# One copy of u for a graph's eight slots, two relus kept on ScalarE, and masks and counts on VectorE, in a two-layer graph network

## The chip, the cores and the metric

The kernel runs on one core of a Trainium2 chip. TensorE (PE in the profile, its weight loads PEld), VectorE (DVE), ScalarE (ACT) and GpSimd (POOL) each work through an instruction queue of their own, in order; SyncE (SP) issues most of the loads and stores. The metric is the device time of one execution in microseconds (us); lower is better.

## The reference, cut to what matters

There are 128 graphs of 128 nodes with 64 features. Layer 0 takes, for each node j, the sum over its neighbours k of a relu of a term of j plus a term of k. Layer 1 is a message pass with a GRU update. Each layer ends in a residual sum and a layer norm.

```python
# layer 0
mask = (adj > 0.0).astype(x.dtype)
h = relu((x @ W1a)[:, :, None, :] + (x[:, :, None, :] - x[:, None, :, :]) @ W1b + b1)
hm = einsum('bjkh,bjk->bjh', h, mask)          # H = 192
x = layernorm(x + hm @ W2 + sum(mask, -1)[..., None] * b2)
# layer 1
m = relu(relu(x @ W1 + b1) @ W2 + b2)
msg = relu(adj @ m)
r, z, n = gru_gates(msg, x)
x = layernorm(x + (1.0 - z) * n + z * x)
```

With u = x(W1a + W1b) + b1 and v = -x W1b, the term is relu(u[j] + v[k]).

## The kernel before

**Work and tiles.** The kernel takes 32 groups of four graphs (`G` = 4). A graph's neighbours are split into two halves of 64 (`K`), and each node's neighbours in a half are numbered by a running count (`ranks`, from the mask by a matmul). A node has eight first slots in each half (`W0` = 8); what goes beyond lies in segments of four (`W1` = 4), which `counts`, `offsets` and `places` lay out in 128 rows a graph. `own` says which node owns a segment row; it comes from `till` (L464), a comparison of a ramp with the running sum of segments, by a matmul of differences (L469) and two copies (L472, L474).

**Gathers.** `pick0` (L518) holds one-hot matrices: which neighbour fills slot c of node j. A gather (L633) is twelve matmuls of 64 rows: two slots (`C` = 2), two halves, and v as the sum of three bf16 pieces b0, b1, b2 (`pieces`, L567 to L576). It adds v of two slots of all 128 nodes to a PSUM tile of 128 x 2 x 2 x 192 that already holds u. ScalarE put it there: a seed (L603) copies u into all four places of the tile. The result is u[j] + v[k]. The first gather of a graph is read by ScalarE, which keeps relu of it in `acc` (L653); the later ones by VectorE, which adds their relu to `acc` (L663).

**How far one seed goes.** One tile is seeded for `CH` = 2 gathers. The second gather uses differences of picks (slot minus the slot two before, L532): it takes the old v out and puts the new one in, so it must wait until the first has been read. Four gathers of a graph take two seeds. The segment rows (t = 1) go by pairs of graphs: one seed from `us` (`over`, L614 and L620) for four gathers, by `pick1`. Three PSUM tiles (`ps_g`) take turns.

**Sums.** GpSimd folds `acc` in two steps and subtracts `nb`, the relu of u for the empty slots (`together`, L683 to L688, once a graph); `joined` (L696) does the segments' first step. `sums` (L708 to L726) turns both to feature rows hmT. `others` makes t4 = degree x b2 + x on GpSimd (L479, L481).

**Tail of a group.** `second` multiplies hmT by W2 (L283, L287), adds t4 (L291) and starts the layer norm: statistics on VectorE (L253, L255), eps, negated mean, power -0.5 and their product on GpSimd (L258 to L264), scale and shift on ScalarE (L268). `turn`, `message1` to `message3`, `gates` and `update` are layer 1; the update's four steps (L363 to L372) run on GpSimd, for the last group on VectorE. In the last group `filler` issues matmuls of zeros to an otherwise unused tile (L277).

**Order.** The order is written out: `TIMETABLE` gives each part of a group a due time per step, with 100000 units for one group, `FIRST` other ones for group 0, `SETUP` those of the constants. All steps are sorted by due time and issued so, each engine's queue in that order; steps of up to four groups alternate. The due times set the order only; waiting is by semaphores. The loads of a group (adjT L396, xT L402, x L404) go out on SP some two groups ahead. Behind the last group a check of the segment counts (L777 to L782) guards a slow path, which doesn't run here.

Of the kernel before, what the change touches and what calls it, by code (L numbers as in the profile page):

```python
# [8 lines left out]
F32 = mybir.dt.float32  # L9
# [6 lines left out]
N = 128  # L16
F = 64
# [7 lines left out]
CH = 2  # L25
# [6 lines left out]
    "load": (-239888,), "masks": (-238156,), "ranks": (-200576, -194850), "degrees": (-228408, -221484),  # L32
    "turned": (-189933, -183749), "counts": (-191910,), "offsets": (-181787, -175193, -172562, -162838, -161741),
    "owners": (820, 6053), "places": (-147612, -144441), "pieces": (-137076, -118201, -110813, -98096),
# [5 lines left out]
    "together3": (3714, 4697, 9068), "second": (29982, 34541, 34541, 44075, 44075, 45808), "turn": (49612, 49612),  # L40
    "message1": (55001, 56214), "message2": (57048, 57570), "message3": (65700, 77281),
    "gates": (83209, 86661, 89400, 92470, 92470, 92470),
    "update": (101744, 120595, 123001, 139151, 150290, 198413, 246921, 250824, 311612),
# [3 lines left out]
    "reduce": (-89041, -82113, -76359, -62977, -60541, -50033, -42948, -38936, -23485, -15405, -15405, -3453),  # L47
    "seed1": (-48740, -15516), "gather1": (-43978, -41686, -35644, -21221, -11810, -3717, 8136, 9311),
    "keep1": (-43301, -6818), "reduce1": (-37237, -25519, -20358, -3084, 8983, 10522),
# [3 lines left out]
SETUP = (-246768, -205868, -187652, -148058, -89840, 21303)  # L53
FIRST = {
    "load": (-190305, -108672), "masks": (-146596,), "ranks": (-129578, -128520), "degrees": (-138361, -133585),
    "turned": (-96218, -93766), "counts": (-124777,), "offsets": (-105877, -105577, -94566, -80587, -71431),
    "places": (-66249, -65974), "pieces": (-99801, -97830, -85303, -54033), "values0": (-105954, -105954, -105954),
    "values1": (-107124, -106310, -106310), "pick0": (-113119, -99973, -97396, -97396), "pick1": (-52074, -45312),
    "over0": (-59699, -52348),
# [4 lines left out]
def adj_resnorm_kernel(  # L64
    ctx: ExitStack,
    tc: tile.TileContext,
    x: bass.AP,
# [17 lines left out]
    NB = x.shape[1]  # L85
# [18 lines left out]
    iota = const.tile([N, N], BF16, name="iota")  # L104
# [4 lines left out]
    wall = const.tile([N, 2, 2 * H], F32, name="wall")  # L109
    b1o = const.tile([N, H], BF16, name="b1o")  # L110
# [37 lines left out]
    def turned_round(out, src):  # L148

        nc.scalar.copy(out[:, :, 0 : H - N], src[:, :, N:H])  # L150
        nc.scalar.copy(out[:, :, H - N : H], src[:, :, 0:N])

    def setup(ps_g, ps_w):
# [10 lines left out]
        for h in range(2):  # L164
            spread(bias[h * F : h * F + 3, 0:H], b1)
# [40 lines left out]
        turned_round(b1o.rearrange("p (c h) -> p c h", c=1), b1r.rearrange("p (c h) -> p c h", c=1))  # L206
# [15 lines left out]
        yield  # L222
        nc.vector.tensor_copy(bias[:, H : H + F], bi[:, 128:H])
        nc.vector.tensor_add(bias[:, H + F : 2 * H], bias[:, H + F : 2 * H], bi[:, 0:128])

# [15 lines left out]
    def tail_parts(s, work, ps_w, n, store):  # L241


        name = s["name"]

# [3 lines left out]
        def layernorm(y, tag, into):  # L249
# [4 lines left out]
            for i in range(n):  # L254
                nc.vector.bn_aggr(mv[:, i, :], stats[:, i, :])  # L255
            yield
            ve = work.tile([N, n], F32, tag="ve" + tag, name=f"ve{tag}_{name}")
            nc.gpsimd.tensor_scalar(ve, mv[:, :, 1], EPS, None, ALU.add)  # L258
            nm = work.tile([N, n], F32, tag="nm" + tag, name=f"nm{tag}_{name}")
            nc.gpsimd.tensor_scalar(nm, mv[:, :, 0], -1.0, None, ALU.mult)  # L260
# [3 lines left out]
            nc.gpsimd.tensor_tensor(nm, nm, rs, ALU.mult)  # L264
# [7 lines left out]
        def filler(n):  # L272

            if name == str(ng - 1):
                p = s["spare"]
                for i in range(n):
                    nc.tensor.matmul(p, ones_h, zeros, start=True, stop=True)  # L277

        def second():
            ps = [ps_w.tile([N, 2, F], F32, tag="w", name=f"pw{name}") for h in range(2)]  # L280
            hm = s["hmT"]
            for i in range(n):
                nc.tensor.matmul(ps[i % 2][:, i // 2, :], hm[:, i // 2, i % 2, :], w2c[:, 0, :], start=i < 2, stop=False)  # L283
            yield
            for i in range(n):
                hs = slice(i % 2 * F, (i % 2 + 1) * F)
                nc.tensor.matmul(ps[i % 2][:, i // 2, :], hm[hs, i // 2, 2, :], w2c[hs, 1, :], start=False, stop=i >= 2)  # L287
            yield
            y = work.tile([N, n, F], F32, tag="y0", name=f"y0_{name}")
            for h in range(2):  # L290
                nc.vector.tensor_add(y[:, h:n:2, :], ps[h], s["t4"][:, h:n:2, :])  # L291
            filler(9)
            yield from layernorm(y, "0", "x1")

        def turn():
            p = ps_w.tile([N, 2, N], F32, tag="w", name=f"pt{name}")
            for i in range(2):
# [3 lines left out]
            s["x1T"] = work.tile([N, 2, N], F32, tag="x1T", name=f"x1T{name}")  # L301
            nc.scalar.copy(s["x1T"], p)

        def message1():
            p = ps_w.tile([N, 2, N], F32, tag="w", name=f"pm{name}")
# [3 lines left out]
            s["m1"] = work.tile([N, 2, N], F32, tag="m1", name=f"m1_{name}")  # L309
            nc.scalar.activation(s["m1"], p, AF.Relu, bias=gb1)  # L310

        def message2():
            p = ps_w.tile([N, n, F], F32, tag="w", name=f"pn{name}")
            nc.tensor.matmul(p, ones_h, each(gb2, n), start=True, stop=False)
            for i in range(2):
                nc.tensor.matmul(p[:, 2 * i : 2 * i + 2, :], s["m1"][:, i, :], gw2, start=False, stop=i == 1)
# [5 lines left out]
        def message3():  # L322
            p = ps_w.tile([N, 2, N], F32, tag="w", name=f"pa{name}")
            for i in range(2):
# [564 lines left out]
```

## Time and profile before

| | |
|---|---|
| median of 3 runs | 984.29 us (983.44 to 986.48) |
| profiled execution: its time | 983.37 us |
| its span, first to last instruction | 981.5 us |
| busy in the span: PE, DVE, ACT, POOL | 898.1, 857.8, 841.0, 889.1 us |
| granted TensorE clock, mean | 0.984 |
| gathers L633 | 9216 matmuls, 481.6 us busy |
| relu and add L663 | 576 x 950 ns |
| seeds L603 from uv, from us | 256 x 807 ns, 64 x 807 ns |
| relus kept L653 | 192 x 810 ns |

A row of the profile names line, engine, operation, output and inputs by the program's names, shape and count, then busy time and the mean of one in ns; in brackets or behind a bar stand the idle time of the engine ahead of it and what ended that. A group is one 32nd of these counts. Timelines give start, length and line, with "x24" for instructions of a kind in a row.

### The profile page before, as it was taken

To read this page: it belongs to the slowest core of one execution; us is meant where nothing else is said; L and a number is where in the kernel's file an instruction comes from. 1 tells how busy PE (TensorE), PEld (TensorE's weight loads), DVE (VectorE), ACT (ScalarE), POOL (GpSimd) and SP (SyncE) were. 2 spreads that over 40 slices of the span, in tenths; PEclk is the share of its full clock that TensorE was granted. 3 is DMA by queue.
4 is the path that set the end of the run, shared out by engine and by line. 5 is a ranking of instruction groups with operands and counts; after the bars stand their busy time and mean duration, and the time that the engine had idled before them with its cause. 6 is when DMAs were issued, how large, how long until landed. Compare 5 with 4: busy or idle time off the path is not lost.

```text
span 981.5 us, 31854 instructions
## 1 busy us (share of the span) xinstructions
PE 898.1 (91%) x13015; PEld 703.1 (72%) x13015; DVE 857.8 (87%) x1617; ACT 841.0 (86%) x1708; POOL 889.1 (91%) x1171
## 2 busy tenths in 40 slices
PE   5789999999999999999999999999999999999984
PEld 2567777777777777777777777777777777777762
DVE  5888999888989989899988898998989998889962
ACT  4878889888889888888988888988888998888863
POOL 4658899999999999999999999999999999999963
PEclk6999999999999999999999999999999999999997
DMA  3000000001010001001000000001011000000000
GB/s 108 13 2 23 24 29 3 29 29 29 28 29 11 21 28 29 29 29 29 3 29 28 29 28 29 8 23 30 28 29 29 22 9 29 28 29 7 8 8 19
DMA packets 21459, 23.86 MB, mean 24 GB/s; under 512 B 4150, under 2 KB 17212, under 8 KB 21308
## 3 DMA queue, kind: packets, MB, share of 16 engines
q1 hardware_dynamic: 21308, 21.78, 7.4%
q8 instruction: 104, 1.70, 0.7%
q14 instruction: 47, 0.39, 0.1%
HBM read 17.57 MB, written 4.19 MB: 22 GB/s over the span
## 4 chain that ended last, share of the span: by engine, by line
PE 42%; POOL 36%; DVE 15%; issue 4%; ACT 2%; DMA 0%; DVEq 0%; SPq 0%; ACTq 0%; POOLq 0%
PE pv L633 19%; DVE acc L663 9%; POOL fs L688 6%; POOL acc L683 5%; POOL acc L696 5%; POOL acc L685 5%; POOL b L576 4%; PE pw L283 3%; PE pu L548 3%; POOL r L570 3%; PE ph L715 2%; PE pm L306 2%; PE pw L287 2%; POOL t L481 2%; DVE stats L253 2%
## 5 line engine op out<-in xcount | busy, mean ns | idle before, releaser
L663 DVE SCALAR_TENSOR_TENSOR acc<-pv,acc 128x768 f32<-128x768 f32 x576 | 534.4, 950 | 80.3 <-PE pv L633 63.7
L633 PE MATMUL pv<-b,pick 64*128 64x192 bf16 x9216 | 481.6, 244 | 37.1 <-DVE acc L663 14.9
L633 PEld LDWEIGHTS <-pick 64*128 64x128 bf16 x9216 | 379.1, 95 | 113.7 <-issue 86.2
L603 ACT COPY pv<-uv 128x768 f32<-128x768 f32 x256 | 204.2, 807 | 11.5 <-DVE acc L663 11.5
L653 ACT ACTIVATE acc<-pv 128x768 f32<-128x768 f32 x192 | 155.5, 810 | 23.9 <-PE pv L633 23.0
L683 POOL TENSOR_TENSOR acc<-acc 128x384 f32<-128x384 f32 x128 | 131.3, 1026 | 16.8 <-DVE acc L663 16.8
L685 POOL TENSOR_TENSOR acc<-acc 128x192 f32<-128x192 f32 x128 | 107.1, 836 | 2.7
L518 DVE TENSOR_TENSOR pick<-rankT,ramp 128x2048 bf16<-128x2048 bf16 x64 | 85.1, 1331 | 0.0
L688 POOL TENSOR_TENSOR fs<-acc,nb 128x192 f32<-128x192 f32 x128 | 75.2, 598 | 0.2
L726 ACT COPY hmT<-ph 128x384 f32<-128x384 f32 x64 | 31.1, 486 | 48.3 <-PE ph L720 48.3
L262 POOL TENSOR_TENSOR rs<-ve,nhalf 128x4 f32<-128x4 f32 x64 | 66.7, 1042 | 0.0
L696 POOL TENSOR_TENSOR acc<-acc 128x384 f32<-128x384 f32 x64 | 64.2, 1004 | 1.9 <-DVE acc L663 1.9
L576 POOL TENSOR_TENSOR b<-r,b 128x768 bf16<-128x768 f32 (+1 forms) x35 | 54.0, 1542 | 11.9 <-ACT b L573 11.9
L548 PE MATMUL pu<-wall,xT 64*128 64x384 f32 x256 | 60.8, 526 | 1.4 <-DVE larger L434 0.6
L614 PE MATMUL pz<-uv,own 128*128 128x192 f32 x256 | 58.9, 353 | 0.7 <-ACT own L474 0.7
L555 ACT COPY uv<-pu 128x384 f32<-128x384 f32 x128 | 55.1, 485 | 4.9 <-PE pu L551 4.8
L603 ACT COPY pv<-us 128x768 f32<-128x768 f32 x64 | 51.6, 807 | 6.9 <-DVE acc L663 6.8
L675 ACT ACTIVATE nb<-uv,npad 128x192 f32<-128x192 f32 x128 | 57.5, 450 | 0.0
L268 ACT ACTIVATE x<-y,nm,rs 128x64 f32<-128x64 f32 x128 | 45.9, 429 | 13.1 <-POOL nm L264 13.1
L570 POOL TENSOR_TENSOR r<-uv,b 128x768 f32<-128x768 f32 x31 | 51.1, 1650 | 3.3 <-ACT b L567 3.3
L414 POOL TENSOR_SCALAR maskT<-adjT 128x512 bf16<-128x512 f32 x32 | 49.1, 1535 | 5.1 <-DMA adjT<-in_adjT_dram 5.1
L715 PE MATMUL ph<-ownT,acc 128*128 128x128 f32 x256 | 42.1, 287 | 11.9 <-POOL acc L696 11.9
(150 smaller groups left out, 1746.4 us busy)
## 6 DMA issues: line engine op xcount, KB each, us to landing
adjT<-in_adjT_dram SPq DMA_DIRECT2D x32, 256.0 KB, 2.8
xT<-in_xT_dram SPq DMA_DIRECT2D x64, 64.0 KB, 2.8
x<-in_x_dram SPq DMA_DIRECT2D x32, 128.0 KB, 2.4
out_dram<-o SPq DMA_DIRECT2D x32, 128.0 KB, 1.7
wab<-in_w_dram SPq DMA_DIRECT2D x2, 96.0 KB, 2.5
bi<-in_b_ih_dram SPq DMA_DIRECT2D x1, 96.0 KB
bias<-in_b_hh_dram SPq DMA_DIRECT2D x1, 96.0 KB
wx<-in_w_hhT_dram SPq DMA_DIRECT2D x2, 48.0 KB, 2.7
```

What stands on the lines that cost most here:

```text
L518: nc.vector.tensor_tensor(s[name][:, rows], s[src].rearrange("p (o g) n -> p o g n", o=1).to_broadcast([N, n, G, N]), ramp[:, first : firs ...
L548: nc.tensor.matmul(ps[h], s["xT"][ks, i, :], wall[ks, i, :], start=True, stop=False)
L570: (nc.vector if g == 0 else nc.gpsimd).tensor_tensor(r[:, gs], v, b[0][:, gs], ALU.subtract)
L576: nc.gpsimd.tensor_tensor(b[2][:, gs], r[:, gs], b[1][:, gs], ALU.subtract)
L603: nc.scalar.copy(v, src.to_broadcast(list(v.shape)))
L633: nc.tensor.matmul(v[:, h, j, :], pick[ks], s[f"b{c}"][ks, gr, :], start=False, stop=c == 2, skip_group_check=True,)
L653: nc.scalar.activation(kept(s, t, i), view(s["pv", t, i, 0]), AF.Relu)
L663: nc.vector.scalar_tensor_tensor(out=a, in0=view(s["pv", t, i, k // CH if t == 0 else 0]), scalar=0.0, in1=a, op0=ALU.max, op1=ALU.add,)
L683: nc.gpsimd.tensor_tensor(f[:, 0], f[:, 0], f[:, 1], ALU.add)
L685: nc.gpsimd.tensor_tensor(f[:, 0, 0], f[:, 0, 0], f[:, 0, 1], ALU.add)
L688: nc.gpsimd.tensor_tensor(fs[:, i % 2], f[:, 0, 0], s["nb", i], ALU.subtract)
L696: nc.gpsimd.tensor_tensor(f[:, 0], f[:, 0], f[:, 1], ALU.add)
```

## The change

- **Seeds.** `CH` is 4: one seed for a graph's four gathers, so four instead of eight a group. The picks of the second to fourth gather are all differences, and one more set of them is computed.
- **Lift.** For graphs 1 and 3 of a group the last gather is not added by VectorE: ScalarE keeps its relu in a tile of its own (`lift`), and GpSimd adds that to `acc`.
- **Sums by pairs.** `together` works on two graphs in one instruction, twice as wide.
- **Mask, counts, layer norm.** The mask, the five counts, eps and the negated mean times the power move from GpSimd to VectorE; the negated mean is no step of its own any more.
- **Till and own.** `till` is the sign of a ramp plus offset, in four ScalarE activations; the two copies of own scale by a half and add a constant column `top`.
- **x.** It is not loaded a second time: the residual enters y by matmuls of xT with the identity; `others` loses its addition. Graphs alternate between the halves of xT, so the two copies of wall become one. Group 0's adjT and xT are loaded from ScalarE's queue ahead of its table load.
- **Update.** The z columns of weights and bias are negated, so that the gate gives 1 - z: y = (tanh - x1)(1 - z) + 2 x1, three steps instead of four, and 2 x1 on ScalarE.
- **Last group.** Its layer 1 runs in two pairs of graphs with parts of their own (`second_a` to `update_a`).
- The due times are all new, and some tiles have other buffer counts (fs, us, nb, acc0, lift).

The diff, without the tables of due times, the halved index ranges of `tail_parts` and the slow path:

```diff
-CH = 2
+CH = 4
+LIFT = (1, 3)
...
-        nc.vector.tensor_add(wall[:, 0, 0:H], wab[:, 0, :], wab[:, 1, :])
-        nc.vector.tensor_scalar_mul(wall[:, 0, H : 2 * H], wab[:, 1, :], -1.0)
-        turned_round(wall[:, 1, :].rearrange("p (c h) -> p c h", c=2), wall[:, 0, :].rearrange("p (c h) -> p c h", c=2))
-        nc.vector.tensor_copy(iota, ips)
+        nc.vector.tensor_add(wall[0:F, 0:H], wab[0:F, 0, :], wab[0:F, 1, :])
+        nc.vector.tensor_scalar_mul(wall[0:F, H : 2 * H], wab[0:F, 1, :], -1.0)
+        for o, c in ((0, slice(N, H)), (H - N, slice(0, N))):
+            k = c.stop - c.start
+            nc.vector.tensor_add(wall[F:N, o : o + k], wab[F:N, 0, c], wab[F:N, 1, c])
+            nc.vector.tensor_scalar_mul(wall[F:N, H + o : H + o + k], wab[F:N, 1, c], -1.0)
+        nc.vector.tensor_scalar(behind, ips, -1.0, -0.5, ALU.mult, ALU.add)
+        nc.vector.tensor_scalar_mul(top, ident[:, 0:1], 0.5)
...
+        nc.gpsimd.tensor_scalar(wm[:, 128:H], wm[:, 128:H], -1.0, None, ALU.mult)
+        nc.gpsimd.tensor_scalar(wx[:, F:128], wx[:, F:128], -1.0, None, ALU.mult)
...
-            yield
             ve = work.tile([N, n], F32, tag="ve" + tag, name=f"ve{tag}_{name}")
-            nc.gpsimd.tensor_scalar(ve, mv[:, :, 1], EPS, None, ALU.add)
-            nm = work.tile([N, n], F32, tag="nm" + tag, name=f"nm{tag}_{name}")
-            nc.gpsimd.tensor_scalar(nm, mv[:, :, 0], -1.0, None, ALU.mult)
+            nc.vector.tensor_scalar(ve, mv[:, :, 1], EPS, None, ALU.add)
+            yield
             rs = work.tile([N, n], F32, tag="rs" + tag, name=f"rs{tag}_{name}")
             nc.gpsimd.tensor_tensor(rs, ve, nhalf[:, 0:n], ALU.pow)
             yield
-            nc.gpsimd.tensor_tensor(nm, nm, rs, ALU.mult)
+            nm = work.tile([N, n], F32, tag="nm" + tag, name=f"nm{tag}_{name}")
+            nc.vector.scalar_tensor_tensor(out=nm, in0=mv[:, :, 0], scalar=-1.0, in1=rs, op0=ALU.mult, op1=ALU.mult)
             yield
             s[into] = work.tile([N, n, F], F32, tag=into, name=f"{into}_{name}")
             for i in range(n):
...
+                nc.tensor.matmul(ps[i % 2][:, i // 2, :], g["xT"][hs, (lo + i) // 2, :], ident[hs, hs], start=False, stop=False)
...
+            s["x2"] = work.tile([N, n, F], F32, tag="x2", name=f"x2{name}")
+            nc.scalar.mul(s["x2"], s["x1"], 2.0)
+            yield
-            side.tensor_tensor(a, s["x1"], t, ALU.subtract)
+            side.tensor_tensor(a, t, s["x1"], ALU.subtract)
             yield
             b = work.tile([N, n, F], F32, tag="ub", name=f"ub{name}")
             side.tensor_tensor(b, a, s["rz"][:, :, F:128], ALU.mult)
             yield
-            c = work.tile([N, n, F], F32, tag="uc", name=f"uc{name}")
-            side.tensor_tensor(c, b, t, ALU.add)
-            yield
             y = work.tile([N, n, F], F32, tag="y1", name=f"y1_{name}")
-            side.tensor_tensor(y, c, s["x1"], ALU.add)
+            side.tensor_tensor(y, b, s["x2"], ALU.add)
             yield
             yield from layernorm(y, "1", "o")
...
-                nc.sync.dma_start(s["adjT"], adjT[:, gs, :])
+                q = nc.scalar if g == 0 else nc.sync
+                q.dma_start(s["adjT"], adjT[:, gs, :])
...
-                    nc.sync.dma_start(s["xT"][h * F : (h + 1) * F], xT[:, g * G + 2 * h : g * G + 2 * h + 2, :])
-                s["x"] = loads.tile([N, G, F], F32, tag="x", name=f"x{g}")
-                nc.sync.dma_start(s["x"], x[:, gs, :])
+                    q.dma_start(s["xT"][h * F : (h + 1) * F], xT[:, g * G + h : (g + 1) * G : 2, :])
...
-                nc.gpsimd.tensor_scalar(s["maskT"], s["adjT"], 0.0, None, ALU.is_gt)
+                nc.vector.tensor_scalar(s["maskT"], s["adjT"], 0.0, None, ALU.is_gt)
...
-                nc.gpsimd.tensor_scalar(up, s["larger"], 1.0 / W1, less - float(W0) / W1, ALU.mult, ALU.add)
+                nc.vector.tensor_scalar(up, s["larger"], 1.0 / W1, less - float(W0) / W1, ALU.mult, ALU.add)
+                yield
...
-                nc.vector.tensor_tensor(
-                    s["till"], each(iota, G), off.rearrange("p (g o) -> p g o", o=1).to_broadcast([N, G, N]), ALU.is_lt
-                )
+                for i in range(G):
+                    nc.scalar.activation(s["till"][:, i, :], behind, AF.Sign, bias=off[:, i : i + 1])
...
-                nc.scalar.copy(s["own"], s["po"])
+                nc.scalar.activation(s["own"], s["po"], AF.Identity, bias=top, scale=0.5)
                 s["own32"] = prep.tile([N, G, N], F32, tag="own32", name=f"own32_{g}")
-                nc.scalar.copy(s["own32"], s["po"])
+                nc.scalar.activation(s["own32"], s["po"], AF.Identity, bias=top, scale=0.5)
 
...
-                nc.gpsimd.tensor_tensor(s["t4"], s["t4"], s["x"], ALU.add)
...
-                v = s["pick0"].rearrange("p (q h c) g n -> p q h c g n", q=2, h=2)
-                for q in range(2):
-                    nc.vector.tensor_tensor(v[:, q, 1], v[:, q, 1], v[:, q, 0], ALU.subtract)
+                for a, b in ((C, 2 * C), (2 * C, W0)):
+                    nc.vector.tensor_tensor(p[:, W0 - C + a : W0 - C + b], p[:, a:b], p[:, a - C : b - C], ALU.subtract)
...
-                        pick, gr = (s["pick1"][:, k and W1 - 1 + k, 2 * i + j, :], 2 * i + j) if t else (s["pick0"][:, C * k + j, i, :], i)
+                        pick, gr = (s["pick1"][:, k and W1 - 1 + k, 2 * i + j, :], 2 * i + j) if t else (s["pick0"][:, k and W0 - C + C * k + j or j, i, :], i)
...
-                    if k:
+                    if k and not (t == 0 and k == nu[0] - 1 and i in LIFT):
...
+        def lift(s, i):
+
+            def part():
+                r = s["lift", i] = main.tile([N, 2, C, H], F32, tag="lift", name=f"lift{s['g']}", bufs=2)
+                nc.scalar.activation(r, view(s["pv", 0, i, 0]), AF.Relu)
+                yield
+
+            return part
+
         def base(s, i):
 
             def part():
-                nb = s["nb", i] = main.tile([N, H], F32, tag="nb", name=f"nb{s['g']}")
-                nc.scalar.activation(nb, s["uv"][:, i, 0:H], AF.Relu, scale=s["npad"][:, i : i + 1])
-                yield
-
-            return part
-
-        def together(s, i):
-            def part():
-                f = kept(s, 0, i)
-                nc.gpsimd.tensor_tensor(f[:, 0], f[:, 0], f[:, 1], ALU.add)
-                yield
-                nc.gpsimd.tensor_tensor(f[:, 0, 0], f[:, 0, 0], f[:, 0, 1], ALU.add)
-                yield
-                fs = made(s, ("fs", i // 2), main, [N, 2, H], F32, tag="fs", name=f"fs{s['g']}")
-                nc.gpsimd.tensor_tensor(fs[:, i % 2], f[:, 0, 0], s["nb", i], ALU.subtract)
+                nb = made(s, ("nb", i // 2), main, [N, 2, H], F32, tag="nb", name=f"nb{s['g']}", bufs=3)
+                nc.scalar.activation(nb[:, i % 2], s["uv"][:, i, 0:H], AF.Relu, scale=s["npad"][:, i : i + 1])
+                yield
+
+            return part
+
+        def together(s, q):
+            def part():
+                f = s["acc0", q]
+                for i in range(2):
+                    if 2 * q + i in LIFT:
+                        nc.gpsimd.tensor_tensor(f[:, i], f[:, i], s["lift", 2 * q + i], ALU.add)
+                        yield
+                nc.gpsimd.tensor_tensor(f[:, :, 0], f[:, :, 0], f[:, :, 1], ALU.add)
+                yield
+                nc.gpsimd.tensor_tensor(f[:, :, 0, 0], f[:, :, 0, 0], f[:, :, 0, 1], ALU.add)
+                yield
+                fs = s["fs", q] = main.tile([N, 2, H], F32, tag="fs", name=f"fs{s['g']}", bufs=2)
+                nc.gpsimd.tensor_tensor(fs, f[:, :, 0, 0], s["nb", q], ALU.subtract)
                 yield
 
             return part
...
-            parts = {"load": loading(s), **prep_parts(s), **tail_parts(s, work, ps_w, G, storer(g))}
+            parts = {"load": loading(s), **prep_parts(s)}
+            if g < ng - 1:
+                parts.update(tail_parts(s, work, ps_w, G, storer(g)))
+            else:
+                early = tail_parts(s, work, ps_w, 2, storer(g), fill=False)
+                parts.update({f"{k}_a": v for k, v in early.items()})
+                parts.update(tail_parts(s, work, ps_w, 2, storer(g, 2), lo=2))
```

More of the change, by code (lines that the diff above doesn't have):

```diff
@@ L54 @@
+SETUP = (-210902, -209161, -159689, -149348, -142856, -97187)
 FIRST = {
[L55 to L58, printed above, removed]
@@ L60 @@
+    "over0": (-92867, -90401),
 }
@@ L272, in filler @@
         def filler(n):
-            if name == str(ng - 1):
-                p = s["spare"]
+            if fill and name == str(ng - 1):
+                p = g["spare"]
                 for i in range(n):
@@ L279, in second @@
         def second():
-            ps = [ps_w.tile([N, 2, F], F32, tag="w", name=f"pw{name}") for h in range(2)]
-            hm = s["hmT"]
+            ps = [ps_w.tile([N, n // 2, F], F32, tag="w", name=f"pw{name}") for h in range(2)]
+            hm = g["hmT"]
             for i in range(n):
-                nc.tensor.matmul(ps[i % 2][:, i // 2, :], hm[:, i // 2, i % 2, :], w2c[:, 0, :], start=i < 2, stop=False)
+                nc.tensor.matmul(ps[i % 2][:, i // 2, :], hm[:, (lo + i) // 2, i % 2, :], w2c[:, 0, :], start=i < 2, stop=False)
             yield
@@ L295, in turn @@
         def turn():
-            p = ps_w.tile([N, 2, N], F32, tag="w", name=f"pt{name}")
-            for i in range(2):
+            p = ps_w.tile([N, n // 2, N], F32, tag="w", name=f"pt{name}")
+            for i in range(n // 2):
                 nc.tensor.transpose(p[:, i, :], s["x1"][:, 2 * i : 2 * i + 2, :], ident)
@@ L760, in adj_resnorm_kernel @@
             for name, times in TIMETABLE.items():
+                if name not in parts:
+                    continue
                 if g == 0 and name in FIRST:
```

130 lines of the change are left out of this document (67 added, 63 removed), and 20 rows, old and new, of the table TIMETABLE.

## The prediction

> **What bounds the kernel now.** First the page's head and its chain of waits, then the stretches by time, then one period of each engine's timeline.
>
> ```profile
> span 981.5 us, 31854 instructions
> PE 898.1 (91%) x13015; PEld 703.1 (72%) x13015; DVE 857.8 (87%) x1617; ACT 841.0 (86%) x1708; POOL 889.1 (91%) x1171
> PE 42%; POOL 36%; DVE 15%; issue 4%; ACT 2%; DMA 0%; DVEq 0%; SPq 0%; ACTq 0%; POOLq 0%
> ```
>
> Four engines lie between 86% and 91%, so shares alone name no bound. The chain of 500 to 600 us, deep in the steady part, repeats every 29.05 us (one group of four graphs). Busy time there, in the order PE, PEld, DVE, ACT, POOL, then the granted clock, DMA share and GB/s:
>
> ```profile
> 500.00:600.00 100.00, 95.03 (x1419) 75.30 (x1420) 91.08 (x163) 90.25 (x184) 96.47 (x123) 1.00 0.07 22
> ```
>
> POOL has 3.5% idle; its timeline tells of what kind:
>
> ```profile
> 498.50 0.23 POOL L258 TENSOR_SCALAR ve<-mv 128x4 f32<-128x4 f32 x1 [0.17 <-DVE mv L255]
> ...
> 500.27 1.66 POOL L685 TENSOR_TENSOR acc<-acc 128x192 f32<-128x192 f32 x1
> ...
> 506.09 1.00 POOL L683 TENSOR_TENSOR acc<-acc 128x384 f32<-128x384 f32 x1
> 507.06 1.51 POOL L414 TENSOR_SCALAR maskT<-adjT 128x512 bf16<-128x512 f32 x1
> 508.53 0.59 POOL L685 TENSOR_TENSOR acc<-acc 128x192 f32<-128x192 f32 x1
> ...
> 510.33 1.65 POOL L570 TENSOR_TENSOR r<-uv,b 128x768 f32<-128x768 f32 x1
> ```
>
> From 492.99 to the same instruction at 522.04 POOL has one wait, the 0.17; the rest are gaps of about 0.07 between small dependent instructions. **POOL's queue is full and sets the 29.05.** PE comes next. Its waits in that period:
>
> ```profile
> 500.39 1.17 PE L633 MATMUL pv<-b,pick 64*128 64x192 bf16 x24 [0.36 <-DVE acc L663]
> ...
> 514.39 0.67 PE L633 MATMUL pv<-b,pick 64*128 64x192 bf16 x12 [0.31 <-ACT acc L653]
> ...
> 516.10 1.00 PE L633 MATMUL pv<-b,pick 64*128 64x192 bf16 x20 [0.22 <-POOL b L576]
> ...
> 521.18 0.55 PE L708 MATMUL ph<-ident,fs 128*128 128x128 f32 x3 [0.17 <-ACT hmT L726]
> 522.14 0.71 PE L715 MATMUL ph<-ownT,acc 128*128 128x128 f32 x4 [0.41 <-POOL acc L696]
> ```
>
> The end of a matmul is modelled, so I count a wait from start to start: 24 gathers take 1.09 undisturbed and 1.62 with the second of these waits, 0.53 lost. In the same way the five lose 0.44, 0.53, 0.29, 0.23 and 0.56; L298 loses 0.21 on x, whose nm POOL makes. Together 2.26: **PE needs 29.05 - 2.26 = 26.8 us a group.**
>
> **The change, engine by engine, per group of four.** Durations are start to start in that period, or a row's mean where they stand alone.
>
> *POOL* loses the mask (1.47), the five counts (1.75 with gaps), x's addition L481 (0.69), uc L369 (0.69), ve and both nm of two layer norms (2 x 0.75), and the four-fold sums L683, L685, L688 (4 x (0.97 + 0.55 + 0.56) = 8.3): 14.4. It gains two lift additions and two first sums of 768 elements (4 x 1.61, by L570 of the same size; in several dimensions no row shows it, bounds 1.61 and two of 384, 1.94; I take 1.61), and two sums and two subtractions of 384 (4 x 0.97): 10.3. So 29.05 - 14.4 + 10.3 = **25.0**. POOL stops being the bound.
>
> *PE* gains four matmuls of x with the identity: eight records like L287, which takes 0.50 for its eight. **27.3**, now the largest.
>
> *ACT* at 90.25% is 26.2. Four seeds go (4 x 0.76 = 3.0), two lift relus come (2 x 0.71). Till comes as four 128x128 activations with a bias from memory. No row has that shape: from 0.25 (x1T L302, 256 wide, without one) to 0.39 (nb L675, 192 wide with one operand from memory); I take 0.33, as x L268 (64 wide with two) steps by 0.33. That is 1.3. Own and own32 gain a bias operand (2 x 0.1: m L310 takes 0.486 against 0.381 of rz at the same width), and 2 x1 costs 0.28. 26.2 - 3.0 + 1.4 + 1.3 + 0.2 + 0.3 = **26.4**: the engine that gives up four seeds is not relieved.
>
> [...]
>
> *DVE* at 91.08% is 26.5. Two additions go (2 x 0.87) and till (1.03). The mask comes: between 0.42 (L199's 0.248 for 192 and 0.181 for 64 elements, carried to 512) and POOL's 1.47; 0.45, since L199 is the same operation on the same engine. Five counts, two ve, two nm: nine tiny ones at 0.1, bounds 0.07 (step of the reduces L432, L434) and 0.16 (their duration): 0.9. The differences of pick0 grow from two of 1024 to one of 1024 and one of 2048 (0.68 to about 1.15): +0.5. 26.5 - 1.7 - 1.0 + 0.45 + 0.9 + 0.5 = **25.6**.
>
> The two engines disturb each other: L685 takes 1.66 at 500.27, where DVE's pick L518 starts at 500.26, and 0.59 at 508.53. Such excesses of POOL sum to 4.6 in the period and stay inside my 25.0, as the picks stay.
>
> [...]
>
> *Waits.* PE's loss on POOL (0.29 + 0.56 + 0.21) should go, since POOL has 3 us free; that on hmT too, since the two ph are no longer neighbours in PE's order (gathers, pu and pz lie between). What stays is 0.44 + 0.53, about 1.0, on DVE and ACT emptying PSUM. Bounds: 0.17, what POOL as the bound loses today, and 2.26, all that PE loses. I take 1.0, as those rows name engines that stay at 25.6 and 26.4. **Period 27.3 + 1.0 = 28.3**; 0.75 saved.
>
> Moved at no cost: uv, values and the transposed x load keep counts; xT (2.8 us to landing) is loaded almost a period ahead of values, and SP loses one load of 128 KB a group. Were that cover gone, values would start up to 2.8 late once, not per group.
>
> *Start.* Before, adjT waits on SP behind weights until 5.77, lands at 8.61, and the mask on POOL is ready for its first reader at 10.2. Now ACT's queue issues it first (ACT starts at 0.73, landing about 3.6), and the mask stands on DVE behind its set-up, which ended L189 at 5.18: ready at 5.7, 4.5 earlier. Behind it group 0 needs about as long as before to its first gather (19.75). The later weights go ahead of group 1's loads on SP: 9.4 us of issues, so its xT lands near 20, when PE first asks for it. I take 4; bounds 0 (xT late by as much) and 5.
>
> *End.* From y at 958.06 to the last o at 978.4 go 20.4 us. Pairs halve x and o (2 x 0.7), spare POOL's ve and nm (2 x 0.6) and make four updates of 0.43 into three of 0.29 (0.85); about 2 more from half-width message and gate steps. That is 5.5; but the second pair follows the first by its own share of ACT and PE, 3 to 4. I take 2; bounds 5 and -1.
>
> **Sum.** 31 periods lie between the first and the last group: 31 x 0.75 = 23.3; with 4 and 2, 29.3. The profiled execution took 983.37 (981.5 of span and 1.9 around it); the median shown is 984.29, 0.9 more. 983.4 - 29.3 = **954**.
>
> **The rivals.**
> *Tight packing* (0.14): PE waits 0.3 a group, nearer POOL's 0.17. Period 27.6, 31 x 1.45 + 6 = 51: 932; with 0.6, 942. Against it: three engines at 91% to 97% of PE.
> *ACT becomes the bound* (0.13): it keeps its idle 2.8 beside 26.4, so 29.2; +0.15 x 31 - 6: 982, or 979 if till is at its low bound. For it: till now stands in ACT's queue ahead of rz and a keep, and pp and a gather wait for those. Against it: 1.5 of those 2.8 are hmT's wait for ph, which waits for POOL.
> *Slower: PE's hand-overs* (0.13). With one tile for four gathers, each but the first waits until DVE or ACT has read the slot before: 3 x 6 = 18 a group against 8 + 6 = 14. If four new waits at L642 cost 0.27 each (today's cost 0.44 and 0.53), they fill the 1.06 that POOL gave back, and hmT's stays: 27.3 + 2.26 = 29.6, 31 x 0.55 - 6 = +11: 994. It decides from 1.95 us of waits a group on. Against it: the order puts another tile's gather or other matmuls between two gathers of one tile.
>
> **How the numbers follow.** The forecast (943 to 970: waits of 0.6 to 1.5) has 0.60. The range 936 to 980 leaves out the slower rival, half of ACT's and a little of the tight one. About 0.3% is what a measurement of this kernel can tell from no change: faster 0.82, same 0.05 (from ACT's rival), slower 0.13.
>
> **What would show it.** POOL's idle rises to 3 us a group; PE is busiest, at 96% or more; waits of L642 on L672 and L662 sum to 1 us a group; the seeds' count halves to 128 on uv; the first gather comes near 15. Wrong: a period above 29, PE idle on L672 by 2 us, POOL still packed (768-wide additions well over 1.61), or till's chain heading ACT's waits.

## The result, and the profile after

| | before | after |
|---|---|---|
| median | 983.87 us (983.43 to 986.48) | 1119.21 us (1113.57 to 1129.58) |
| ratio | | 1.138, 95% interval 1.129 to 1.147 |
| profiled execution, its span | 983.37, 981.5 us | 1117.02, 1115.2 us |
| granted TensorE clock, mean | 0.984 | 0.908 |
| one group in the steady part | 29.05 us | 34.1 us |

The forecast of 954 us is wrong in sign: the change makes the kernel slower by 135 us. Of all executions below only one, the 1115.7 us of "nm later", lies more than 1.5% above the fastest of its kernel, and it enters no ratio. The page's head and its chain of waits, after:

```profile
span 1115.2 us, 32118 instructions
PE 970.2 (87%) x13276; PEld 761.9 (68%) x13276; DVE 984.6 (88%) x1859; ACT 859.4 (77%) x1808; POOL 770.2 (69%) x600
PE 52%; DVE 26%; issue 11%; ACT 9%; POOL 2%; ACTq 0%; DVEq 0%; POOLq 0%
```

GpSimd has left the chain (36% before, 2% now), as forecast. In its place stand VectorE (15% before, 26% now) and "issue". DVE's busy time rose from 857.8 to 984.6 us, although the sum of its work was to fall. 500 to 600 us, columns as before:

```profile
500.00:600.00 100.00, 88.42 (x1222) 69.90 (x1221) 91.55 (x167) 78.50 (x166) 69.76 (x53) 0.91 0.06 18
```

No engine is full, and the clock, 1.00 here before, is 0.91. One group's timeline tells why (start, length; the bracket is the idle time ahead):

```profile
522.75 0.17 DVE L264 TENSOR_SCALAR ve<-mv 128x4 f32<-128x4 f32 x1
...
522.83 1.22 DVE L528 TENSOR_TENSOR pick<-rankT,ramp 128x2048 bf16<-128x2048 bf16 x1
523.00 1.92 POOL L267 TENSOR_TENSOR rs<-ve,nhalf 128x4 f32<-128x4 f32 x1 [2.56 <-DVE ve L264]
...
524.12 0.92 PE L623 MATMUL pz<-uv,own 128*128 128x192 f32 x4
524.91 1.79 POOL L703 TENSOR_TENSOR acc<-acc,lift 128x768 f32<-128x768 f32 x1
524.96 1.76 DVE L270 SCALAR_TENSOR_TENSOR nm<-mv,rs 128x4 f32<-128x4 f32 x1 [0.76 <-POOL rs L267]
526.64 1.81 DVE L672 SCALAR_TENSOR_TENSOR acc<-pv,acc 128x768 f32<-128x768 f32 x2
...
527.64 1.15 PE L642 MATMUL pv<-b,pick 64*128 64x192 bf16 x12 [2.60 <-DVE acc L672]
```

Read it downwards. The pick, right behind ve on VectorE, stretches GpSimd's power rs to 1.92 (1.02 elsewhere in the trace). nm waits 0.76 for rs; then, a hair behind GpSimd's addition L703, it lasts 1.76 for four columns and ends where L703 ends (524.91 + 1.79 = 526.70; 524.96 + 1.76 = 526.72). The nm of the other layer norm takes 0.15 at 509.75, just as a GpSimd addition ends. Only then come the relu-additions that free the PSUM tile, and TensorE has stood for 2.60. Over the whole execution, in rows of count, busy time, mean in ns and idle time ahead:

```profile
L270 DVE SCALAR_TENSOR_TENSOR nm<-mv,rs 128x4 f32<-128x4 f32 x62 | 65.4, 1056 | 24.0 <-POOL rs L267 24.0
L642 PE MATMUL pv<-b,pick 64*128 64x192 bf16 x9216 | 514.1, 255 | 123.4 <-DVE acc L672 107.8 <-ACT acc L662 10.1 <-ACT pv L612 2.2
```

What the clock makes of that, microsecond by microsecond in the same stretch (first PE, then PEld, DVE, ACT, POOL, clock):

```profile
524.00:525.00 1.00, 1.00 (x10) 0.66 (x5) 0.24 (x4) 0.17 (x1) 1.00 (x2) 1.00 0.74 259
525.00:526.00 1.00, 0.04 (x1) 0.06 (x1) 1.00 (x1) 0.00 (x0) 1.00 (x1) 1.00 0.21 60
526.00:527.00 1.00, 0.00 (x0) 0.00 (x0) 1.00 (x2) 0.24 (x1) 0.92 (x2) 0.86 0.02 8
527.00:528.00 1.00, 0.36 (x6) 0.36 (x7) 1.00 (x2) 1.00 (x4) 1.00 (x1) 0.50 0.00 0
...
533.00:534.00 1.00, 1.00 (x11) 0.99 (x9) 0.91 (x2) 0.58 (x2) 0.71 (x1) 0.73 0.00 0
534.00:535.00 1.00, 1.00 (x24) 0.89 (x24) 1.00 (x2) 0.71 (x3) 0.93 (x1) 1.00 0.07 16
```

The gap halves the clock for about 7 us, in which the twelve matmuls of a gather take 1.07 to 1.15 instead of 0.60 to 0.67, and this comes back every group. A second place in the same trace is an operation with one input, tot, beside another L703; it too ends with it:

```profile
507.99 1.81 POOL L703 TENSOR_TENSOR acc<-acc,lift 128x768 f32<-128x768 f32 x1 [3.75 <-ACT lift L684]
508.02 1.81 DVE L456 TENSOR_SCALAR tot<-nseg_all 128x4 f32<-128x4 bf16 x1
```

**Theory A, locked VectorE.** As I read it, while GpSimd runs a long operation on SBUF (L703, 1.8 us), a small one of VectorE on SBUF doesn't proceed (nm 1.76, tot 1.81 for four columns); the relu-additions queued behind nm start late, at 526.64, and TensorE first idles for 2.60 and then runs about 7 us at half clock. **Rival B** is that of the prediction, the hand-overs of one PSUM tile to four gathers. **Rival C**: the clock is low for another reason, and the gaps follow from it.

### The profile page after: what moved, and what is told of

Read it like the earlier page. It is cut to its first block, busy times and chain, and to the rows that moved or that the text cites. A ratio compares the mean times of both kernels' runs of the same rounds, so it can differ in the third digit from the quotient of the medians.

```text
span 1115.2 us, 32118 instructions
## 1 busy us (share of the span) xinstructions
PE 970.2 (87%) x13276; PEld 761.9 (68%) x13276; DVE 984.6 (88%) x1859; ACT 859.4 (77%) x1808; POOL 770.2 (69%) x600
## 4 chain that ended last, share of the span: by engine, by line
PE 52%; DVE 26%; issue 11%; ACT 9%; POOL 2%; ACTq 0%; DVEq 0%; POOLq 0%
PE pv L642 25%; DVE acc L672 15%; ACT acc L662 6%; PE pz L623 4%; DVE tot L456 3%; PE pw L289 2%; PE pu L557 2%; PE pm L315 2%; ACT pv L612 2%; PE ph L730 2%; PE ph L737 2%; PE pt L307 1%; PE pw L293 1%; PE pr L497 1%; PE ph L742 1%
## 5 line engine op out<-in xcount | busy, mean ns | idle before, releaser
L642 PE MATMUL pv<-b,pick 64*128 64x192 bf16 x9216 | 514.1, 255 | 123.4 <-DVE acc L672 107.8
L642 PEld LDWEIGHTS <-pick 64*128 64x128 bf16 x9216 | 410.1, 98 | 223.1 <-issue 207.2
L672 DVE SCALAR_TENSOR_TENSOR acc<-pv,acc 128x768 f32<-128x768 f32 x512 | 475.8, 949 | 74.7 <-PE pv L642 65.0
L703 POOL TENSOR_TENSOR acc<-acc,lift 128x768 f32<-128x768 f32 x64 | 115.5, 1805 | 112.0 <-ACT lift L684 112.0
L267 POOL TENSOR_TENSOR rs<-ve,nhalf 128x4 f32<-128x4 f32 (+1 forms) x66 | 93.0, 1410 | 118.3 <-DVE ve L264 113.6
L705 POOL TENSOR_TENSOR acc<-acc 128x768 f32<-128x768 f32 x64 | 117.4, 1834 | 5.0
L718 POOL TENSOR_TENSOR acc<-acc 128x384 f32<-128x384 f32 x64 | 89.6, 1400 | 45.2 <-DVE acc L672 45.2
L612 ACT COPY pv<-uv 128x768 f32<-128x768 f32 x128 | 103.9, 812 | 3.4 <-DVE acc L672 3.4
L274 ACT ACTIVATE x<-y,nm,rs 128x64 f32<-128x64 f32 x128 | 46.1, 430 | 78.5 <-DVE nm L270 78.5
L541 DVE TENSOR_TENSOR pick<-pick 128x1024 bf16<-128x1024 bf16 x64 | 105.6, 1651 | 0.0
L270 DVE SCALAR_TENSOR_TENSOR nm<-mv,rs 128x4 f32<-128x4 f32 (+1 forms) x66 | 66.6, 1009 | 28.2 <-POOL rs L267 28.2
L710 POOL TENSOR_TENSOR fs<-acc,nb 128x384 f32<-128x384 f32 x64 | 74.2, 1160 | 2.5
L707 POOL TENSOR_TENSOR acc<-acc 128x384 f32<-128x384 f32 x64 | 67.7, 1058 | 5.0
L579 POOL TENSOR_TENSOR r<-uv,b 128x768 f32<-128x768 f32 x31 | 56.7, 1830 | 0.9 <-ACT b L576 0.8
L684 ACT ACTIVATE lift<-pv 128x768 f32<-128x768 f32 x64 | 53.1, 830 | 0.1
```

Of the source, the lines that this page charges most:

```text
L267: nc.gpsimd.tensor_tensor(rs, ve, nhalf[:, 0:n], ALU.pow)
L541: nc.vector.tensor_tensor(p[:, W0 - C + a : W0 - C + b], p[:, a:b], p[:, a - C : b - C], ALU.subtract)
L612: nc.scalar.copy(v, src.to_broadcast(list(v.shape)))
L642: nc.tensor.matmul(v[:, h, j, :], pick[ks], s[f"b{c}"][ks, gr, :], start=False, stop=c == 2, skip_group_check=True,)
L672: nc.vector.scalar_tensor_tensor(out=a, in0=view(s["pv", t, i, k // CH if t == 0 else 0]), scalar=0.0, in1=a, op0=ALU.max, op1=ALU.add,)
L703: nc.gpsimd.tensor_tensor(f[:, i], f[:, i], s["lift", 2 * q + i], ALU.add)
```

## The experiments

Held time in the table is a sum that I work out from the rows by form of VectorE's picks, nm, ve, counts, mask and till: count times what the mean is above the undisturbed value (small ones 0.16, picks of 1024, 1536 and 2048 elements 0.68, 0.95 and 1.21, mask 0.41, till 1.03 us). Each ratio is to the kernel before as timed beside that run.

| kernel | us | ratio to before | VectorE held, us | clock | period |
|---|---|---|---|---|---|
| before | 983.9 | | 12 | 0.984 | 29.1 |
| after | 1119.2 | 1.138 [1.129, 1.147] | 177 | 0.908 | 34.1 |
| nm on GpSimd | 974.8 | 0.990 [0.986, 0.994] | 64 | 0.987 | 28.7 |
| nm, tot, npad on GpSimd | 972.5 | 0.988 [0.982, 0.993] | 50 | 0.985 | 28.6 |
| loads on SP, built on the last | 972.1 | 0.988 [0.985, 0.992] | 49 | 0.985 | 28.6 |
| nm, tot, npad and up on GpSimd | 969.4 | 0.986 [0.984, 0.988] | 78 | 0.985 | 28.6 |
| nm and all counts on GpSimd | 1017.6 | 1.036 [1.033, 1.039] | 80 | 0.971 | 29.0 to 31.7 |
| zeros in TensorE's gap | 1046.3 | 1.062 [1.057, 1.068] | 122 | 0.988 | 31.1 |
| before, ve and nm on VectorE | 1050.3 | 1.066 [1.060, 1.072] | 34 | 0.951 | 30.1 to 32.9 |
| additions in halves | 1050.5 | 1.068 [1.063, 1.073] | 133 | 0.981 | 31.3 |
| no lift | 1048.0 | 1.066 [1.064, 1.067] | 127 | 0.992 | 31.3 |
| second pick later | 1066.0 | 1.084 [1.081, 1.087] | 133 | 0.950 | 31.6 |
| nm later | 1087.9, 1115.7 | | 176 | 0.941 | 30.8 to 34.2 |
| nm later, counts on GpSimd | 1133.4 | 1.152 [1.149, 1.156] | 143 | 0.901 | 34.1 |

**1. nm back on GpSimd**, all else as changed.

```diff
-nc.vector.scalar_tensor_tensor(out=nm, in0=mv[:, :, 0], scalar=-1.0, in1=rs, op0=ALU.mult, op1=ALU.mult)
+nc.gpsimd.tensor_scalar(nm, mv[:, :, 0], -1.0, None, ALU.mult)
+nc.gpsimd.tensor_tensor(nm, nm, rs, ALU.mult)
```

> The changed kernel with one part undone: the negated mean times the power (L270) goes back from VectorE to GpSimd, in two steps right behind the power. Theory A (locked VectorE): in the changed kernel this tiny instruction waits 0.76 us for GpSimd's power and is then held 1.76 us while GpSimd's 768-wide addition L703 runs; the relu-additions behind it are late, TensorE idles 2.6 us in one piece and its granted clock falls to half for about 7 us in each group of 34.1 us. Without it the gap goes, the clock returns to 0.97 or more, the period falls to 28.5 to 31 us: 945 to 1020 us in all. Theory B (hand-overs): with one tile for four gathers TensorE has to wait for readers anyway; the waits move to other gathers, the period stays above 32.5, time above 1070 us.

974.8 us. 500 to 600 us:

```profile
500.00:600.00 100.00, 96.07 (x1451) 77.03 (x1450) 91.90 (x191) 91.87 (x199) 93.21 (x80) 1.00 0.07 21
```

TensorE is at 96% and the clock at 1.00. Taking back one tiny instruction, twice a group, recovers all of the loss and more: 144 us. The hand-overs are all still there, and yet the gathers' wait for the relu-additions falls from 107.8 to 10.4 us, so B is no main cause:

```profile
L643 PE MATMUL pv<-b,pick 64*128 64x192 bf16 x9216 | 474.1, 245 | 24.5 <-DVE acc L673 10.4 <-ACT acc L663 10.3 <-ACT pv L613 2.2
```

rs is still held by the pick (1.94), but on GpSimd's queue nothing that TensorE needs soon stands behind it.

**2. tot and npad on GpSimd too** (`vector` to `gpsimd` in two lines).

> As the kernel before it, and the last two counts (tot L456 and npad L459) go back to GpSimd as well. Theory A: tot is held 1.8 us by L703 once a group, so up to 1.7 us a group more is saved, 0 to 50 us under the run with the negated mean alone. Theory B: no difference within 1%.

972.5 us, 0.2% under run 1, which does not tell A from B: in run 1 tot no longer meets a GpSimd addition and takes 0.17 on the mean, so there was nothing to take back. (In run 11, where nm is hardly held, tot is held again, 1.41 on the mean.)

**3. Zeros in the gap**, ten matmuls behind the second pz. They write to the PSUM tile of pz, and this kernel does not keep the seeds in it whole; the other engines run as many instructions as after the change.

```diff
+if i0 == 2:
+    for i in range(FILL):
+        nc.tensor.matmul(p, ones_h, zeros[...], start=False, stop=True, ...)
```

> The changed kernel with ten matmuls of zeros (384 columns, 0.16 us each at full clock, added to the PSUM tile of pz) behind the second pz of each group, where TensorE now idles 2.6 us; nothing else is moved. If the low clock follows from the idle piece (part of theory A), the clock returns to 0.97 or more although VectorE's wait stays: about 3 us a group less, 1020 to 1060 us in all. If the clock is low for another reason (theory C: load, heat, the mean activity), it stays near 0.9 and the time at 1110 us or more.

1046.3 us at a clock of 1.00 in the steady part:

```profile
500.00:600.00 100.00, 93.62 (x1344) 73.19 (x1340) 91.32 (x184) 83.68 (x179) 83.36 (x58) 1.00 0.08 22
```

C falls: work without use in the gap brings the clock back, and 73 of the 135 us come with it. Not all 73 need be the clock's, for tot is no longer held here either (0.17 on the mean, 1.25 after), and the shares are not separated. nm is held as before (1.76 at 501.43), and the rest of the loss stays: ScalarE's x still waits 71.0 us in all for nm (78.5 after).

**4. The kernel before, with eps and nm on VectorE**, nothing else of the change.

> The kernel before with one part of the change alone: eps and the negated mean times the power of both layer norms on VectorE. GpSimd, which was the full queue there, loses about 1.4 us a group. By the reasoning of my prediction (GpSimd's load is what counts) the period falls from 29.05 to about 28: 940 to 965 us. Theory A: the negated mean waits on VectorE for GpSimd's queue and is held by its additions there too (0.6 to 1.0 us each, shorter than the 1.8 of the changed kernel), so little or nothing is gained: 975 to 1050 us.

1050.3 us, the upper end of A's range: this part of the change alone costs 66 us, although it takes work off the engine that was the bound. nm takes 0.68 in this group (0.39 on the mean), held by a 256-wide addition of GpSimd, and TensorE waits for x:

```profile
507.25 1.04 POOL L371 TENSOR_TENSOR y<-uc,x 128x256 f32<-128x256 f32 x1
507.63 0.68 DVE L263 SCALAR_TENSOR_TENSOR nm<-mv,rs 128x4 f32<-128x4 f32 x1
...
509.17 0.47 PE L297 MATMUL pt<-ident,x 128*128 128x128 f32 x1 [1.37 <-ACT x L267]
```

TensorE then runs at about half pace until 512.6: the twelve matmuls of the gather at 511.56 take 1.14 (0.67 at 515.02). The gap was 1.37 us, with another of 0.59 at 506.04 shortly before. The hold, 0.5 us here, is only part of nm's delay: rs was ready at 507.28, but nm stood behind a pick that VectorE worked on until 507.72.

**5. Order alone**: nm behind two relu-additions.

```diff
-"second": (15724, 16020, 19642, 25835, 25867, 26896)
+"second": (15724, 16020, 19642, 25835, 31000, 31001)
```

> The changed kernel, with nothing but the due time of one step altered: nm of the first layer norm stays on VectorE, but stands behind two relu-additions of the gathers instead of ahead of them. In the changed kernel those two additions start at 526.64, though their picks and counts before nm end at 524.2. Theory A (locked VectorE, nm ahead of the additions): the additions start about 2.4 us earlier, TensorE's gap after pz falls below 1 us, the granted clock stays near 1.00, and the time is 970 to 1015 us. A rival that blames the amount of work on VectorE, or the hand-overs of one PSUM tile to four gathers (theory B), changes nothing by an order: 1090 to 1125 us.

A's number was missed: 1087.87 us in the profiled run, 1115.73 in the other. The rival's range of 1090 to 1125 is far nearer; it is runs 1 and 11 that speak against the amount of work and the hand-overs. The two relu-additions start at 521.92 straight behind the reductions, as expected, and the gap on them is gone. But the hold has moved to the next small operations:

```profile
522.71 1.81 POOL L703 TENSOR_TENSOR acc<-acc,lift 128x768 f32<-128x768 f32 x1
523.65 0.89 DVE L270 SCALAR_TENSOR_TENSOR nm<-mv,rs 128x4 f32<-128x4 f32 x1
524.46 0.16 DVE L447 TENSOR_SCALAR up<-larger 128x4 f32<-128x4 f32 x1
524.59 1.80 POOL L705 TENSOR_TENSOR acc<-acc 128x768 f32<-128x768 f32 x1
524.65 1.77 DVE L450 TENSOR_SCALAR rnd<-up 128x4 f32<-128x4 f32 x1
525.40 0.33 PE L307 MATMUL pt<-ident,x 128*128 128x128 f32 x1 [1.80 <-ACT x L274]
```

nm ends with L703 (524.52 and 524.54), rnd with L705 (526.39 and 526.42), and TensorE now waits 1.80 for x. That wait is nm's: rs was ready at 522.73, nm started 0.92 later, behind the two relu-additions, and was held another 0.7. rnd delays the third relu-addition, and no run shows what that costs. So A had to be widened: not nm's place alone, but whichever small operation meets a long GpSimd operation.

**6. GpSimd's 768-wide additions in two of 384.**

> The changed kernel with GpSimd's 768-wide additions (lift and first sum) each issued as two of 384; nm stays on VectorE and where it was. Theory A with holds that last as long as the GpSimd instruction under way: nm is held 1.0 us at most instead of 1.76, tot too, TensorE's gap shrinks from 2.6 to below 2, and a part of the loss goes: 1010 to 1090 us, with the granted clock above 0.93. If VectorE were held by the total of GpSimd's work and not by one instruction: 1105 to 1125 us. GpSimd itself pays about 4 x 0.3 us a group, which it has.

1050.5 us, as A expected:

```profile
502.06 1.94 POOL L704 TENSOR_TENSOR acc<-acc,lift 128x384 f32<-128x384 f32 x2
502.11 0.95 DVE L270 SCALAR_TENSOR_TENSOR nm<-mv,rs 128x4 f32<-128x4 f32 x1 [0.76 <-POOL rs L267]
...
503.99 0.67 PE L642 MATMUL pv<-b,pick 64*128 64x192 bf16 x12 [1.55 <-DVE acc L672]
```

The same work in shorter pieces halves the hold: nm ends at 503.06, halfway through the 1.94 of the two additions, with the first of them. The gap of 1.55 does not slow TensorE: the twelve matmuls behind it take 0.67.

**7. The second pick later**, built on 2: it held the power rs, so it was put behind the two relu-additions (its due time -176688 became -168500).

> Built on the kernel with nm, tot and npad on GpSimd (972.5 us). One due time more: the second pick of the 8-wide round, which stood straight behind ve on VectorE and held GpSimd's power for 0.9 us (1.94 instead of 1.04), stands behind the two relu-additions. If that hold is what keeps x late (TensorE waits 0.3 for x twice a group), the power takes 1.04, x starts 0.9 earlier, and the period falls by 0.2 to 0.5 us: 957 to 968 us, close to the 954 forecast. If those waits only move to the next hand-over: 969 to 976 us.

1066.0 us, 94 more than without it. rs takes 1.04, as wanted, but the pick is now held beside GpSimd's L704 (1.78 at 513.97) and up behind it beside L706 (1.76 at 515.68): 3.5 us between two relu-additions where run 2 has up alone, 1.37. My expectation had asked only what the pick holds, not what would hold the pick.

**8. The first group's loads on SP**, built on 2.

> Built on the kernel with nm, tot and npad on GpSimd (972.5 us). The first group's adjT and xT are loaded by SP behind weights, as in the kernel before, instead of by ACT's queue. If the earlier start is worth what the prediction gave it, 4 us: 975 to 978 us. If the 5 us are lost again before the first pw, as the trace of the changed kernel has it (56.4 against 56.7): 971 to 974 us, with the first gather 4 to 5 us later and the first pw within 1 us.

972.1 us, and it doesn't tell what it was meant to: by the due times adjT goes ahead of the weights on SP (0.73), and only xT is late, by 5.3 us, at 6.47. The first gather is at 14.35 as in 2. It shows that xT had as much time in hand.

**9. nm and all counts on GpSimd**, built on 2.

> The changed kernel with nm and all five counts (up, rnd, nseg, tot, npad) on GpSimd again; ve, mask and everything else as changed. Theory A, widened after the run with nm later: what is held is any small operation on SBUF that VectorE has in its queue while GpSimd runs a 768-wide addition (rnd took 1.77 us there, ending with that addition), and the relu-additions behind it start later by that much. With seven of the nine gone from VectorE, only ve and the picks can be held: the period is 28.0 to 28.6 and the time 958 to 973 us, at most that of nm, tot and npad alone (972.5). A theory of loads: GpSimd gets 25.0 + 3 = 28 us a group and fills up, so it is slower than 972.5: 976 to 990 us.

1017.6 us: both ranges missed. GpSimd isn't full (92.6%); the picks are held longer (29 us instead of 2 on the two of rankT, 20 instead of 1 on the larger difference), and periods between 29.0 and 31.7 follow one another. The moved counts shift GpSimd's additions against the picks; which of them does it stays open.

**10. nm later, counts on GpSimd.**

> The kernel with nm later (1087.9 us), and its five counts on GpSimd again; nm stays on VectorE, behind two relu-additions. Tells whether a held nm is harmless once nothing waits behind it that TensorE needs. Widened theory A: rnd no longer adds its 1.77 us ahead of the third relu-addition, but nm itself still ends with GpSimd's addition (0.9 us): 985 to 1040 us. If nm on VectorE was the whole cause, whatever its place: 1075 to 1115 us.

1133.4 us, slower than the change itself. GpSimd now does up and rnd ahead of L703, so L703 starts only 0.35 before nm instead of 0.94 (run 5); nm is held 1.47, to the end of L703, and its reader x is what TensorE waits for:

```profile
500.69 1.80 POOL L703 TENSOR_TENSOR acc<-acc,lift 128x768 f32<-128x768 f32 x1
501.04 1.47 DVE L270 SCALAR_TENSOR_TENSOR nm<-mv,rs 128x4 f32<-128x4 f32 x1
...
503.37 0.47 PE L307 MATMUL pt<-ident,x 128*128 128x128 f32 x1 [2.40 <-ACT x L274]
```

A gap of 2.40, and about half pace until 509: the gathers' twelve matmuls at 504.44 and 507.02 take 1.14 (0.67 at 500.31). The rival that nm on VectorE hurts in any place, at 1075 to 1115, is nearer than A's 985 to 1040: no place tried for nm on VectorE was good, and the additions behind it are only one of two ways in which a held nm reaches TensorE.

**11. No lift**: all twelve relu-additions on VectorE, two of GpSimd's four 768-wide additions gone.

> The changed kernel without the two kept relus and their two 768-wide GpSimd additions: all twelve relu-additions of the 8-wide round are on VectorE again; nm and counts stay on VectorE. By loads VectorE gets 2 x 0.87 = 1.7 us a group more beside 31 of 34.1 busy, and ScalarE gets 1.4 less: 1115 to 1170 us. Theory A: GpSimd's long additions fall from four to two a group, nm behind the power finds GpSimd free or in a 768-wide first sum one time in two; VectorE's held time falls by 2 to 3 us: 1000 to 1090 us, below the changed kernel in spite of the greater load.

1048.0 us: 71 us faster with more work on the engine that seemed overloaded, as A expected, though VectorE's held time falls by 1.6 us a group and not by 2 to 3. nm takes 0.20 on the mean, the clock is 1.00, and VectorE is now the bound:

```profile
500.00:600.00 100.00, 88.17 (x1314) 69.61 (x1308) 96.86 (x195) 79.45 (x172) 67.67 (x51) 1.00 0.08 23
```

**12. up on GpSimd too**, built on 2.

> Built on the kernel with nm, tot and npad on GpSimd (972.5 us): up, the only small operation that VectorE still held there (1.17 us on the mean instead of 0.16), goes to GpSimd too; rnd and nseg stay on VectorE. Theory A by the sum of held time: 32 x 1.0 us of holding go, part of it beside waits, and GpSimd pays 32 x 0.3, which it has: 962 to 972 us. If the order of GpSimd's additions against VectorE's picks decides, as the run with all counts on GpSimd suggests (1017.6 with picks held longer), rnd is held in up's place or the picks are: 974 to 1020 us.

969.4 us (968.99 to 970.79), the best version found, 1.4% under before. A's number is met, but not by its reason: rnd is held in up's place, as the other answer had it,

```profile
L451 DVE TENSOR_SCALAR rnd<-up 128x4 f32<-128x4 f32 x32 | 54.0, 1688 | 0.0
```

and it costs nothing there: TensorE's gathers wait 7.1 us in all for the relu-additions (8.4 in 2), and the period is 28.6 as in 2. The 3 us to run 2 are in the start (first pw at 56.4 instead of 59.9); the intervals of the two ratios overlap, and run 8 has its first pw at 57.3 with up on VectorE, so they are not shown to be up's. With run 4 (34 us held, 66 us lost) this says that the sum of held time does not set the time; who waits behind it does.

## Why the prediction was wrong, step by step

Two terms failed: the cost of the nine small operations on VectorE, forecast at 0.9 us a group, and TensorE's waits, forecast at 1.0. By the rows after, the small operations take 142.7 us in 32 groups, 4.5 each, and the gathers' wait for the relu-additions is 107.8 us, 3.4 a group, with a halved clock behind it.

- **"nine tiny ones at 0.1, bounds 0.07 ... and 0.16" failed.** nm takes 1056 ns on the mean and tot 1250. The bounds came from two operations of that size, the reduces, that read PSUM; after the change those take at most 0.167, and the relu-additions, which read PSUM too, at most 0.959. nm, tot, up and rnd read and write SBUF, and each was seen at 1.7 to 1.8 beside a GpSimd addition (nm 1.76 and tot 1.81 after, rnd 1.77 in run 5, up 1.76 in run 7).
- **"DVE 25.6" failed with it**: 91.55% of 34.1 are 31.2, and held time, 177 us in 32 groups, is 5.5 of that; 81 of the 177 are the picks', for which the prediction had no hold either. In run 12, 92.87% of 28.6 are 26.6.
- **"Such excesses of POOL ... stay inside my 25.0"** was one-sided. I counted what VectorE's picks take from GpSimd, and not the reverse, though the change gives GpSimd four operations of 1.8 us a group and VectorE nine new small ones. In the traces nm, tot and rnd end within 0.03 us of the GpSimd addition that started before them (nm at 526.72 and L703 at 526.70, tot at 509.83 and L703 at 509.80, rnd in run 5 at 526.42 and L705 at 526.39).
- **The added wait was not priced.** nm on VectorE waits for GpSimd's power with the relu-additions queued behind it: 24.0 us in all, and the hold on top. I had moved ve and nm by durations only. Run 4 shows that this edit alone turns 984 into 1050.
- **"waits about 1.0" failed, and the clock was missing from the sum.** One wait of 2.60 halves the clock for 7 us; nothing in the prediction let TensorE's 27.3 grow. Filling the gap was worth 73 us (run 3).
- **The slower rival** had the right side with the wrong mechanism: waits of L642 on L672 are PE's largest on another engine (107.8 us), but not by the number of hand-overs (run 1).
- **What held.** With nm and the counts that matter off VectorE (run 12), TensorE's 97.11% of 28.6 are 27.8 a group (27.3 forecast) and ScalarE's 91.95% are 26.3 (26.4). As changed, the mask took 0.414 (0.45), till's four 1.29 (1.3), the lift additions 1.80 (1.61, bound 1.94).
- **A sum.** The rival in which ScalarE becomes the bound gives 979 "if till is at its low bound". With four activations at 0.25, the low row, the same sum gives 973; 979 would take till at 1.2, a term that no run shows: the four took 1.29.
- **Start: 4 forecast, 0.3 found.** The mask is done at 5.4 (5.7 forecast) and the first gather at 14.33 (15), but the first pw is at 56.4 against 56.7. In between, among other waits, TensorE waits 1.89 at 28.25 on VectorE, whose biases stand at 21.2 to 25.3 ahead of the relu-additions, and 1.29 at 30.61, with 36 matmuls of gathers in 3.07 after it. **End: 2 forecast, 0.8 found**, from the last pw but one to the end: 51.9 before, 51.1 after.
- **From 954 to run 2's 972.5:** 30 periods of 28.65 instead of 28.3 (10.5), a first pw at 59.9 instead of 52.7 (7) and 1 at the end make 18.5. That is where the rest of the forecast gain went, once nm is out of the way.

## What to carry to other kernels

Price a moved instruction by what runs beside it on the partner engine, and by what stands behind it in its new in-order queue: a 0.15-us step that waits for GpSimd can cost 2.5 us ahead of the step that frees PSUM. A small link of a chain between GpSimd operations can stay on GpSimd if nothing urgent queues behind it there (nm: 144 us), but moving more is no rule (up, rnd and nseg as well cost 45 over run 2). Look at VectorE's and GpSimd's timelines side by side before giving either a long operation. A TensorE gap can cost more than its length (2.60 brought 7 us at half clock, 1.55 and 1.80 none), so look at the clock by the microsecond.

## What the hardware showed that I had not expected

- A 4-column VectorE operation on SBUF was held to the end of a GpSimd addition that started before it, even with one input (tot, rnd, up: 1.76 to 1.81); the relu-additions, which read PSUM, were not (0.94 to 0.96 in the same stretches). Nor was every one on SBUF: after the change the statistics of the layer norm, which read and write SBUF, never take more than 0.23 and 0.18 (the four at 92.01 take 0.60, in the middle of GpSimd's L579 from 90.56 to 93.19, and 0.59 at 529.70 with GpSimd idle), and nseg takes 0.16 at 531.56 in the middle of GpSimd's power (530.86 to 531.88). In these traces, then, what was held depended on the operation and on what GpSimd ran beside it.
- After the gap of 2.60 the clock was 0.50. A gather's twelve matmuls then took 1.07 to 1.15 instead of 0.60 to 0.67; by the same mark (1.14) TensorE ran at about half pace after 2.40 (run 10), and in run 4 after 1.37 with 0.59 shortly before. Behind gaps of 1.55 (run 6) and 1.80 (run 5) they took 0.67. Full pace came back about 5.8 us (as changed), 5.5 (run 10) and 3.5 (run 4) after the end of the gap. What besides the length decides was not settled.
- A change in the order of one step, a pick, moved the whole kernel by 94 us (run 7), and one kernel can run with changing periods (29.0 to 31.7 in run 9).
